# Autocorrelation beside key and value projections: two corrections moved from VectorE to GpSimd and ScalarE, and PSUM banks handed around

## The chip, the cores and the metric

The kernel runs on one core of one Trainium2 chip. A core has five engines with their own instruction queues: TensorE (PE, with PEld for its weight loads) multiplies matrices and writes to PSUM; VectorE (DVE), ScalarE (ACT) and GpSimd (POOL) work on data in SBUF, and the first two on PSUM as well; SyncE (SP) issues nearly all transfers here. PSUM has eight banks of 128 partitions by 512 fp32 numbers. Every engine takes its instructions in a fixed order and waits at an instruction until what it needs is there. The metric is the device time of one execution in microseconds. The kernel before takes 3332.24 us (median of three runs, 3330.26 to 3340.0).

## The reference

The input is `x` of 8 x 256 x 1024 and a context `ctx` of the same shape, all fp32. Four residual steps follow each other, each on the normalised `x` and each with a gate:

1. Autocorrelation attention of the normalised `x` (queries) with `ctx` (keys and values). For each of the 8 x 1024 columns: `corr = ifft(fft(q) * conj(fft(k))).real` along the 256 positions, the 11 largest lags with a softmax over them, and `out = sum_i w_i * v[min(lag_i + pos, 255)]`. A position that runs past the end reads the last position of `v`.
2. A linear layer with a low-rank update chosen per token among four ranks.
3. Grouped-query attention with rotary embedding (32 query heads, 8 key and value heads of 128), with keys and values projected from `ctx`.
4. A linear layer with a low-rank update through an orthogonal Fourier transform.

## The kernel before

The batch is done in two passes of four (`NPASS`, `BP`). A pass runs the autocorrelation with the key and value projections of step 3 beside it (in pass 0 also the folding of step 4's weights), then the linear layer of step 2 (`lora_ffn`), attention, and the last linear layer. In the profile the autocorrelation stages lie at 0 to 375 us (pass 0) and 1715 to 2060 us (pass 1).

**Autocorrelation.** `autocorrelation` (L383) treats 8 units per pass (4 sequences x 2 halves of 512 columns), one per call of `turn` (L472), and one more turn that only finishes. The transforms are matmuls with 128 x 128 matrices, after folding the 256 positions into sums and differences: `sums` (L448) makes `qe, qo` from the normalised x and `ke, ko` from the context `cn`, four adds on POOL (L460 to L463). The fold is written for a sequence shifted by one position, so the last position, which every overrun reads, counts too much: `end` (128 x 512, the last position of `ctx` broadcast to all partitions by a transfer, L445) is taken away from `ke` twice (L466, on DVE), and for the values it is put back in row 0 of the spectrum `kr` (L498, on DVE, one partition by 512). PE reads `ke` first at the start of the next turn (`dft`, L411).

A turn, in the order in which it is written: transfers for the next unit; spectra of `ke, ko`, copied from PSUM by ACT (`kr, kn, ki`); spectra of `qe, qo`, which `products` (L423) multiplies with the key spectra in four DVE instructions out of PSUM (L427 to L430) and joins in two POOL instructions (L431 to L435); the values' odd spectra, copied by ACT (`vr, vi`, L495 and L496); L498; then, for the unit of the turn before, eight transposes of its lag weights `both` on PE (L512, tiles `pt`), their copies `wt` by ACT, and two more rounds of spectra and `products` (`er, ei`, then `odr, odi`); `sums` for the next unit; and at the end the inverse transforms: `correlation` (L556) of this unit, `back` (L525) of the unit before (matmuls L531, added to x by DVE, L370), and `lags` (L567), which finds the largest lags on DVE (its masked weights, L583, read two SBUF tiles) and scales on ACT (L587). Two POOL instructions (L552, L553) make `both`.

**The work beside it.** `fill(n)` takes n steps of `keys_values` (L719): a step is eight matmuls of 128x128 by 256 (L796), half of one of the seven products of a Strassen form. A product is gathered in a bank of `ps_kv` and combined by DVE or ACT (`combine`, L223). A finished key tile is turned by `rope` (L709): three DVE instructions (L714 to L716), the first two into a tile `rope` of which there is one, then a POOL add (L717), then a store. In the first group of pass 0 the sums of weights (`wv_s`), and in later groups sums of the context (`cx_t`), are POOL adds too (L155, L159).

**PSUM.** In this stage: `ps_dft` 4 banks (spectra and `back`), `ps_cor` 1, `ps_out` 1 (the transposes `pt`), `ps_kv` 2, in all eight.

**Order.** The instructions of each engine are put in order by a planner when the program is built: the written order counts, but an instruction that the planner holds to be ready goes ahead of one that it holds not to be. The order is fixed before the program runs. On POOL, for instance, the adds of `sums` stand between those of `products`.

Of the kernel before, what the change touches and what calls it, by code (L numbers as in the profile page):

```python
# [11 lines left out]
F32 = mybir.dt.float32  # L12
U8 = mybir.dt.uint8
I32 = mybir.dt.int32
AF = mybir.ActivationFunctionType
ALU = mybir.AluOpType
AX = mybir.AxisListType
PSUM = bass.MemoryType.PSUM

P = 128  # L20
B, S, D = 8, 256, 1024
# [4 lines left out]
HALF = 512  # L26
# [20 lines left out]
def flamingo_kernel(ctx: ExitStack, tc: tile.TileContext, a: dict, out: bass.AP):  # L47
    nc = tc.nc
# [25 lines left out]
    tab_q = const.tile([P, 2, S], F32, name="tab_q")  # L74
# [306 lines left out]


    def autocorrelation(p, xt, pools, beside, late):  # L383
        c1, w1, w2, ps_dft, ps_cor, ps_out = pools

        def fill(n):
            for _ in range(n):
# [60 lines left out]
        def sums(b, cols, cn, end):  # L448

            xn = big_tile("xn", [2, HALF], "xn")  # L450
            for i, lin in enumerate(norms[b]):
                nc.scalar.activation(
                    xn[:, i, :],
                    xt[b * 2 + i][:, cols],
                    AF.Identity,
                    bias=lin[:, 1:2],
                    scale=lin[:, 0:1],
                )
            qe, qo, ke, ko = one("qe"), one("qo"), one("ke"), one("ko")
            nc.gpsimd.tensor_add(ke, cn[:, 0, :], cn[:, 1, :])  # L460
            nc.gpsimd.tensor_sub(ko, cn[:, 0, :], cn[:, 1, :])
            nc.gpsimd.tensor_add(qe, xn[:, 0, :], xn[:, 1, :])
            nc.gpsimd.tensor_sub(qo, xn[:, 0, :], xn[:, 1, :])  # L463


            nc.vector.scalar_tensor_tensor(ke, end, -2.0, ke, ALU.mult, ALU.add)  # L466
            return b, cols, end, qe, qo, ke, ko


# [2 lines left out]
        def turn(this, before, coming):  # L472


            after = None
            if this:
                b, cols, end, qe, qo, ke, ko = this
                if coming:
                    coming = loads(coming)
                kr_ps, ki_ps = dft((KCE, ke)), dft((KSE, ko), (NYQ, ke))  # L480


                kr, ki, kn = sb("kr"), sb("ki"), sb("kn")
                nc.scalar.copy(kr, kr_ps)
                nc.scalar.copy(kn, kr_ps)
                nc.scalar.activation(ki, ki_ps, AF.Copy, scale=pair)
                nc.scalar.copy(kn[0:1, :], ki_ps[0:1, :])
                re, im = sb("re"), sb("im")
                products(spectrum((CE, SE), (qe, qo)), kr, ki, kn, re, im, False)
                fill(2)  # L490

            if this:
                vr_ps, vi_ps = dft((KCO, ko)), dft((KSO, ke))
                vr, vi = sb("vr"), sb("vi")
                nc.scalar.copy(vr, vr_ps)  # L495
                nc.scalar.copy(vi, vi_ps)  # L496

                nc.vector.scalar_tensor_tensor(  # L498
                    kr[0:1, :], end[0:1, :], 2.0 * S, kr[0:1, :], ALU.mult, ALU.add
                )  # L500
                fill((1 if p == 0 else 2) if before else 6 if p == 0 else 2)
            last = not this
            if before:
                if last:
                    fill(3)
                b_cols, b_tiles, (bkr, bki, bkn, bvr, bvi, both) = before

                wt = []
                for t in range(2):
                    pt = ps_out.tile([P, HALF], F32, tag="out", name="pt")  # L510
                    for c in range(4):
                        nc.tensor.transpose(pt[:, c * P : (c + 1) * P], both[:, t, c, :], ident)  # L512
                    wt.append(one(f"wt{t}"))
                    nc.scalar.copy(wt[t], pt)
                    fill(2 if last else 1)
                er, ei = sb("re"), sb("im")
                products(spectrum((CE, SE), wt), bkr, bki, bkn, er, ei, True)
                fill(2 if last else 1)
                odr, odi = one("odr"), one("odi")
                products(spectrum((CO, SO), wt[::-1]), bvr, bvi, bvr, odr, odi, True)  # L520
                fill(3 if last else 2)
            if this and coming:
                after = sums(*coming)

            def back(l):  # L525


                if before:
                    po = ps_dft.tile([P, HALF], F32, tag="dft", name="po")
                    for i, (k, sp) in enumerate(((0, er), (3, odi)) if l else ((1, ei), (2, odr))):  # L530
                        nc.tensor.matmul(po, inv2[:, k, :], sp, start=(i == 0), stop=(i == 1))  # L531
                    residual(b_tiles[0][:, b_cols], po, tg_x[0])
                    residual(b_tiles[1][:, b_cols], po, tg_x[0] if l else ntg_x[0])
                    fill(1 - l)

            if last:
                back(0)
                back(1)
                return None, None
            w = big_tile("xn", [4, S], "w")  # L540
            cor = correlation(re, im, 0)
            fill(1)
            back(0)
            cor += correlation(re, im, 2)
            for c in range(2):
                lags(w[:, c, :], cor[c])
            fill(1)
            back(1)
            for c in range(2, 4):
                lags(w[:, c, :], cor[c])  # L550
            both = big_tile("xn", [2, 4, P], "both")
            nc.gpsimd.tensor_add(both[:, 0], w[:, :, 0:P], w[:, :, P:S])  # L552
            nc.gpsimd.tensor_sub(both[:, 1], w[:, :, 0:P], w[:, :, P:S])  # L553
            return after, (cols, xt[b * 2 : b * 2 + 2], (kr, ki, kn, vr, vi, both))
# [151 lines left out]
                pass  # L706


    def rope(dst, x, cos, sin, pool):  # L709

        H = P // 2
        t = pool.tile([P, 2, S], F32, tag="rope", name="rope", bufs=1)
        tab = lambda t: t.unsqueeze(1).to_broadcast([t.shape[0], 2, S])
        nc.vector.tensor_mul(t[0:H], x[H:P], tab(sin[H:P, :]))  # L714
        nc.vector.tensor_mul(t[H:P], x[0:H], tab(sin[0:H, :]))
        nc.vector.tensor_mul(dst, x, tab(cos))  # L716
        nc.gpsimd.tensor_add(dst, dst, t)  # L717

    def keys_values(n, groups, pools, tab):  # L719
# [3 lines left out]
        w1, w2, ps_kv = pools  # L723
# [57 lines left out]
        for u in range(4):  # L781
# [4 lines left out]
            for r in SEVEN:  # L786
# [16 lines left out]
                if done:  # L803
                    c, (i, j) = done
                    if kind == "wk":
                        kT = out_tile(c)
                        rope(kT, c, tab[:, 0, :], tab[:, 1, :], w1)
                        place = kT_d.rearrange("(q l i) p t -> q i p l t", l=2, i=2)
                        nc.sync.dma_start(
                            place[i_u, i, :, :, t0 + j * S : t0 + (j + 1) * S], kT  # L810
                        )
                    else:
                        r0, c0 = t0 + j * S, i_u * HALF + i * S
                        nc.sync.dma_start(
                            v_d[r0 : r0 + S, c0 : c0 + S].rearrange("(t p) d -> p t d", p=P), c
                        )
# [33 lines left out]
    def attention(p, xt, gq, go, keep, norms, xops, ahead):  # L850
        with (
# [115 lines left out]
            def queries(step, qT):  # L967

                wops, xo = wq[step], xops[step[0]]
                tiles = {}  # L970
                for r in SEVEN:
                    ps = ps_mm.tile([P, 2, S], F32, tag="mm", name="ps_q")
                    for l in range(2):
                        for c in range(KH):
                            nc.tensor.matmul(  # L975
                                ps[:, l, :],
                                wops[r][:, l, c, :],
                                xo[r][:, c, :],
                                start=(c == 0),
                                stop=(c == KH - 1),  # L980
                            )
                    done = combine(r, ps, tiles, lambda tag: half(tag, 1), lambda ps: ps)
                    if done:
                        qT[done[1]] = half("qT", 7)
                        rope(qT[done[1]], done[0], tab_q[:, 0, :], tab_q[:, 1, :], w1)
                    yield

            def outputs(step, ops):
# [209 lines left out]
            qT = {}  # L1198
# [5 lines left out]
            end = len(steps) - 1  # L1204
# [21 lines left out]
            for k, step in enumerate(steps):  # L1226
# [44 lines left out]
                qT = following  # L1271
# [76 lines left out]
    for p in range(NPASS):  # L1348
        ga, gb = ("a", "b") if p % 2 == 0 else ("b", "a")
        xt = [xpool.tile([P, D], F32, tag="x", name="x") for t in range(TT)]  # L1350
        with (
# [4 lines left out]
            tc.tile_pool(name="kv2", bufs=2, reuse_waits="tile") as kw2,  # L1356
            tc.tile_pool(name="ac_dft", bufs=4, space=PSUM) as ps_dft,
            tc.tile_pool(name="ac_cor", bufs=1, space=PSUM) as ps_cor,
            tc.tile_pool(name="ac_out", bufs=1, space=PSUM) as ps_out,
            tc.tile_pool(name="kv_ps", bufs=2, space=PSUM) as ps_kv,  # L1360
        ):

            tab = kw1.tile([P, 2, S], F32, name="tab")
# [15 lines left out]
            if p == 0:  # L1379
# [2 lines left out]
            autocorrelation(  # L1382
                p,
                xt,
                (c1, aw1, aw2, ps_dft, ps_cor, ps_out),
                steps,
                lambda: load_x(range(2, TT)),
            )
# [183 lines left out]
```

## Time and profile before

| | us |
|---|---|
| median of three runs | 3332.24 |
| the three runs | 3330.26, 3332.24, 3340.0 |
| the profiled execution | 3340.92 |
| its span, first to last instruction | 3339.1 |
| PE busy in it | 3267.4 |
| PE busy in 0 to 375, of 375 | 353.7 |
| PE busy in 1715 to 2060, of 345 | 326.2 |

A timeline line gives the start and the duration in us, the engine, the source line, the operation with output and inputs, the count, and in brackets the idle time of the engine before it with what ended it. "issue" there means that the profile shows nothing that was waited for. Of the windows view, a line gives the busy time (and number of instructions) of PE, PEld, DVE, ACT and POOL, then the granted PE clock, the busy share of the DMA engines and GB/s.

### The profile page before, as it was taken

The page shows a single profiled execution, that of the slowest core. Times are in us where ns is not written, and L with a number is a line of the kernel's source. Part 1 is how long each engine was busy: PE and PEld are TensorE (multiplying, and loading weights), DVE is VectorE, ACT ScalarE, POOL GpSimd, SP SyncE. Part 2 cuts the span into 40 slices and gives each one's busy share as a digit, 9 for nine tenths or more (in the row PEclk, how much of TensorE's full clock was granted, in tenths as well). Part 3 has the DMA queues.
Part 4 walks back from the last instruction along what each step waited for, and adds up shares of the span by engine and source line. Part 5 has one row for each costly group of instructions (what it writes and reads, how often), then busy time and mean ns, then how long its engine had stood idle before and what let it go on. Part 6 is the DMA issues. An engine that isn't in the chain of part 4 may idle for free. (4 is left out here: it accounts for less than half of the span.)

```text
span 3339.1 us, 39371 instructions
## 1 busy us (share of the span) xinstructions
PE 3267.4 (98%) x13456; PEld 2405.0 (72%) x13456; DVE 2221.3 (67%) x4305; ACT 1051.6 (31%) x2555; POOL 1404.9 (42%) x1181
## 2 busy tenths in 40 slices
PE   8999899999999999999999999999999999999999
PEld 6677456777677777775456677568888888888874
DVE  7787657777776655565647686456666767666773
ACT  1332111433333433334113332115343434334420
POOL 4554111323332474576344442112454454454572
PEclk9999999999999999999999999999999999999999
DMA  7534615333433354554354435043555455555551
GB/s 280 175 115 125 235 65 186 130 134 129 145 124 130 132 208 145 183 195 162 115 190 130 138 117 171 7 158 101 168 175 167 160 167 172 166 168 176 171 192 51
DMA packets 215781, 505.55 MB, mean 151 GB/s; under 512 B 25076, under 2 KB 102900, under 8 KB 215582
## 3 DMA queue, kind: packets, MB, share of 16 engines
q1 hardware_dynamic: 214430, 498.84, 44.2%
q0 software_dynamic: 1152, 4.19, 0.3%
q8 instruction: 108, 1.77, 0.2%
q14 instruction: 91, 0.75, 0.1%
HBM read 394.96 MB, written 108.00 MB: 151 GB/s over the span
## 5 line engine op out<-in xcount | busy, mean ns | idle before, releaser
L717 POOL TENSOR_TENSOR qT<-qT,rope 128x512 f32<-128x512 f32 x128 | 170.1, 1329 | 789.9 <-DVE qT L716 750.8
L975 PE MATMUL ps_q<-xn,wq 128*128 128x256 f32 x1920 | 428.9, 379 | 0.0
L975 PEld LDWEIGHTS ps_q<-xn,wq 128*128 128x128 f32 x1920 | 364.8, 190 | 50.5 <-PE po L677 0.5
L1145 ACT ACTIVATE s<-s,nmx 128x256 f32<-128x256 f32 x512 | 255.9, 500 | 245.0 <-DVE nmx L1142 244.8
L1140 DVE COPY_PREDICATED s<-keep,ps_s 128x512 f32<-128x512 uint8 x256 | 184.8, 727 | 156.0 <-PE ps_s L1131 155.1
L975 PE MATMUL ps_q<-xn_t,wq 128*128 128x256 f32 x1280 | 285.6, 379 | 0.0
L370 DVE SCALAR_TENSOR_TENSOR x<-po,tg,x 128x512 f32<-128x512 f32 x248 | 177.3, 743 | 139.3 <-PE po L1319 44.7
L975 PEld LDWEIGHTS ps_q<-xn_t,wq 128*128 128x128 f32 x1280 | 243.2, 190 | 33.1
L1172 ACT COPY wT<-pt 128x512 f32<-128x512 f32 x256 | 138.8, 586 | 361.8 <-PE pt L1166 361.8
L1131 PE MATMUL ps_s<-kT,qT 128*128 128x256 f32 x1024 | 247.9, 379 | 0.0
L1177 PE MATMUL av<-wT,v 128*128 128x256 f32 x1024 | 246.0, 382 | 1.7 <-ACT wT L1172 1.6
L1154 ACT ACTIVATE s<-s,tot 128x256 f32<-128x256 f32 x512 | 230.1, 497 | 40.6 <-DVE tot L1152 40.5
L1177 PEld LDWEIGHTS av<-wT,v 128*128 128x128 f32 x1024 | 191.4, 190 | 54.8 <-issue 22.2
L1067 PE MATMUL po<-wo,oI 128*128 128x256 f32 x896 | 214.7, 379 | 2.0 <-issue 1.2
L1131 PEld LDWEIGHTS ps_s<-kT,qT 128*128 128x128 f32 x1024 | 191.8, 190 | 25.1 <-issue 0.5
L1004 PE MATMUL po<-wo,oT 128*128 128x512 f32 x448 | 201.6, 593 | 0.0
L1067 PEld LDWEIGHTS po<-wo,oI 128*128 128x128 f32 x896 | 168.7, 190 | 25.6 <-issue 2.0
L1185 ACT COPY oT<-av 128x512 f32<-128x512 f32 x128 | 75.0, 586 | 353.9 <-PE av L1177 352.4
L1142 DVE TENSOR_REDUCE nmx<-s 128x2 f32<-128x512 f32 x256 | 173.2, 682 | 6.9
L1067 PE MATMUL po<-wo,oT 128*128 128x256 f32 x672 | 172.1, 382 | 1.9 <-DVE co L1082 0.3
L253 POOL TENSOR_TENSOR x<-x,part 128x512 f32<-128x512 f32 x48 | 68.3, 1423 | 247.1 <-ACT part L252 247.1
L1004 PEld LDWEIGHTS po<-wo,oT 128*128 128x128 f32 x448 | 83.0, 191 | 83.2 <-issue 74.8
(290 smaller groups left out, 6407.1 us busy)
## 6 DMA issues: line engine op xcount, KB each, us to landing
wo<-wo_d SPq DMA_DIRECT2D x144, 512.0 KB, 4.6
wq<-in_wq_dram SPq DMA_DIRECT2D x104, 512.0 KB, 3.5
wq<-wq_d SPq DMA_DIRECT2D x96, 512.0 KB, 3.3
wo<-in_wo_dram SPq DMA_DIRECT2D x56, 512.0 KB, 3.5
wo_d<-fine_t SPq DMA_DIRECT2D x56, 512.0 KB, 3.4
wo<-wo_d SPq DMA_DIRECT2D x96, 256.0 KB, 3.4
w<-w_d SPq DMA_DIRECT2D x36, 512.0 KB, 5.3
wo<-in_wo_dram SPq DMA_DIRECT2D x72, 256.0 KB, 3.3
```

The lines of the kernel that those rows point to most:

```text
L370: nc.vector.scalar_tensor_tensor(xs, ps, g, xs, ALU.mult, ALU.add)
L717: nc.gpsimd.tensor_add(dst, dst, t)
L975: nc.tensor.matmul(ps[:, l, :], wops[r][:, l, c, :], xo[r][:, c, :], start=(c == 0), stop=(c == KH - 1),)
L1004: nc.tensor.matmul(po, ops[r][:, h, t * P : (t + 1) * P], wops[r][:, h, :], start=(h == 0), stop=(h == 1),)
L1067: nc.tensor.matmul(po, left[r2][:, h, :], w[:, h, :], start=(h == 0), stop=(h == 1))
L1131: nc.tensor.matmul(ps[:, t, :], qT[i, n][:, l, t * P : (t + 1) * P], kT[:, n * S : (n + 1) * S], start=True, stop=True,)
L1140: nc.vector.copy_predicated(s, keep[b], ps)
L1142: nc.vector.tensor_reduce(nmx, s, AX.X, ALU.max, negate=True)
L1145: nc.scalar.activation(s[:, t, :], s[:, t, :], AF.Exp, bias=nmx[:, t : t + 1], accum_out=tot[:, t : t + 1],)
L1154: nc.scalar.activation(s[:, t, :], s[:, t, :], AF.Copy, scale=tot[:, t : t + 1])
L1172: nc.scalar.copy(wT[i], pt)
L1177: nc.tensor.matmul(av[:, i, :], kv[step][1][:, n * 2 + c, :], wT[i][:, c, :], start=(c == 0), stop=(c == 1),)
```

## The change

- The last position is taken away from `ke` by two instructions in place of L466: ACT scales `end` by -2 in place, and POOL adds it to `ke`. For row 0 of `kr`, in place of L498, ACT makes `back_end` (a new tile of 128 x 512, row 0 used) as `end` times -S, which is 2S times the position, and POOL adds it to row 0 of `kr`.
- The transposes `pt` get their banks from `ps_dft` (still 4 banks); `ps_out` is gone.
- `ps_kv` has three banks in place of two.
- `rope` takes the number of its buffers: two for the keys, one for the queries, as before.

The whole diff:

```diff
 def autocorrelation(p, xt, pools, beside, late):
-    c1, w1, w2, ps_dft, ps_cor, ps_out = pools
+    c1, w1, w2, ps_dft, ps_cor = pools
...
     nc.gpsimd.tensor_sub(qo, xn[:, 0, :], xn[:, 1, :])
-    nc.vector.scalar_tensor_tensor(ke, end, -2.0, ke, ALU.mult, ALU.add)
+    nc.scalar.activation(end, end, AF.Copy, scale=-2.0)
+    nc.gpsimd.tensor_add(ke, ke, end)
     return b, cols, end, qe, qo, ke, ko
...
     nc.scalar.copy(vr, vr_ps)
     nc.scalar.copy(vi, vi_ps)
-    nc.vector.scalar_tensor_tensor(
-        kr[0:1, :], end[0:1, :], 2.0 * S, kr[0:1, :], ALU.mult, ALU.add
-    )
+    back_end = one("back_end")
+    nc.scalar.activation(back_end[0:1, :], end[0:1, :], AF.Copy, scale=-1.0 * S)
+    nc.gpsimd.tensor_add(kr[0:1, :], kr[0:1, :], back_end[0:1, :])
...
     for t in range(2):
-        pt = ps_out.tile([P, HALF], F32, tag="out", name="pt")
+        pt = ps_dft.tile([P, HALF], F32, tag="dft", name="pt")
...
-def rope(dst, x, cos, sin, pool):
+def rope(dst, x, cos, sin, pool, bufs):
     H = P // 2
-    t = pool.tile([P, 2, S], F32, tag="rope", name="rope", bufs=1)
+    t = pool.tile([P, 2, S], F32, tag="rope", name="rope", bufs=bufs)
...
-        rope(kT, c, tab[:, 0, :], tab[:, 1, :], w1)
+        rope(kT, c, tab[:, 0, :], tab[:, 1, :], w1, 2)
...
-        rope(qT[done[1]], done[0], tab_q[:, 0, :], tab_q[:, 1, :], w1)
+        rope(qT[done[1]], done[0], tab_q[:, 0, :], tab_q[:, 1, :], w1, 1)
...
     tc.tile_pool(name="ac_dft", bufs=4, space=PSUM) as ps_dft,
     tc.tile_pool(name="ac_cor", bufs=1, space=PSUM) as ps_cor,
-    tc.tile_pool(name="ac_out", bufs=1, space=PSUM) as ps_out,
-    tc.tile_pool(name="kv_ps", bufs=2, space=PSUM) as ps_kv,
+    tc.tile_pool(name="kv_ps", bufs=3, space=PSUM) as ps_kv,
...
-        (c1, aw1, aw2, ps_dft, ps_cor, ps_out),
+        (c1, aw1, aw2, ps_dft, ps_cor),
```

## The prediction

> **What bounds the kernel now.** I read the page first: engines, then the windows of the stages, then PE's timeline inside them, then whoever ended its idle time.
>
> ```profile
> PE 3267.4 (98%) x13456; PEld 2405.0 (72%) x13456; DVE 2221.3 (67%) x4305; ACT 1051.6 (31%) x2555; POOL 1404.9 (42%) x1181
> ...
> 0.00:375.00 375.00, 353.70 (x1357) 256.70 (x1358) 274.64 (x668) 102.76 (x182) 181.61 (x149) 0.98 0.51 174
> 375.00:420.00 45.00, 35.11 (x119) 17.18 (x117) 37.88 (x84) 6.20 (x12) 1.26 (x1) 0.92 0.86 302
> 1715.00:2060.00 345.00, 326.22 (x1272) 239.54 (x1271) 247.75 (x616) 96.87 (x174) 159.12 (x125) 0.97 0.42 139
> ```
>
> PE is the bound: it works 98% of the span, and the change neither adds nor removes a matmul. So the change can only alter PE's idle time, 21.3 us in the first autocorrelation stage (375 - 353.7) and 18.8 in the second (345 - 326.2), and the matmuls that run slowly after an idle stretch. PE's timeline shows where:
>
> ```profile
> 77.76 3.75 PE L796 MATMUL ps_v<-wv,cx 128*128 128x256 f32 x8 [4.05 <-issue]
> ...
> 130.28 1.91 PE L411 MATMUL dft<-qo,mats 128*128 128x512 f32 x2 [5.06 <-DVE x L370]
> ...
> 219.53 1.99 PE L796 MATMUL ps_k<-cx,wk 128*128 128x256 f32 x8 [1.12 <-DVE k L716]
> ...
> 1732.56 6.43 PE L796 MATMUL ps_k<-cx,wk 128*128 128x256 f32 x16 [4.54 <-issue]
> ...
> 1781.71 3.07 PE L796 MATMUL ps_k<-cx,wk 128*128 128x256 f32 x8 [3.66 <-DVE k L716]
> ...
> 1906.05 3.78 PE L796 MATMUL ps_k<-cx,wk 128*128 128x256 f32 x8 [6.34 <-DVE v L244]
> ```
>
> Eight of these matmuls take 1.89 us elsewhere and sixteen 3.62, so an idle stretch of 3.7 us or more is paid again, in part, in slow matmuls; one of 1.1 (at 219.53) is not. The releaser is DVE, which frees the key and value banks. Why it was late is told by the correction L466 and one place in the timeline:
>
> ```profile
> L466 DVE SCALAR_TENSOR_TENSOR ke<-end,ke x16: 673/1215/6619, 26.0 to 1982.2; 128x512 f32<-128x512 f32 x16
> ...
>   POOL ke L460: 66.2, 15
> ```
>
> ```profile
> 1896.88 1.27 POOL L460 TENSOR_TENSOR ke<-cn 128x512 f32<-128x512 f32 x1
> ...
> 1898.18 6.62 DVE L466 SCALAR_TENSOR_TENSOR ke<-end,ke 128x512 f32<-128x512 f32 x1 [7.97 <-POOL ke L460]
> ...
> 1899.33 2.48 POOL L159 TENSOR_TENSOR cx_t<-cx,cx_t 128x512 f32<-128x512 f32 x2
> ...
> 1901.76 2.48 POOL L159 TENSOR_TENSOR cx_t<-cx_t,cx 128x512 f32<-128x512 f32 x2
> ...
> 1905.92 0.67 DVE L244 TENSOR_TENSOR v<-ps_v,u 128x512 f32<-128x512 f32 x1
> ```
>
> DVE stands at L466 for POOL, 66.2 us in 15 waits. Here it waits 7.97 us for `ke`, and then, with its input there, the instruction takes 6.62 us instead of 0.69, until POOL's run of adds is over. Behind it queue three combinations of `ps_v` that PE needs.
>
> **The change part by part.**
>
> *L466 leaves DVE.* DVE is freed of the 66.2 us of waits and of 24.4 us of L466 itself (its 16 durations added up). That time counts only where PE waited on it. At 1732.56 DVE had waited 10.65 us in L466 before the combination that frees the bank; at 1781.71, 3.64 us and then 1.76 in the instruction; at 1906.05 as quoted; at 219.53, 2.75 and 1.75. Without L466 each of these combinations is through before PE asks for the bank: at 1728.0 by 0.6 us (the product ends at 1724.6, L244 and the three rope instructions take 2.8), at 1778.05 by 1.8, at the others by more. Each stall is worth its idle time and what the next groups took over their normal spacing: 4.54 + 2.8 = 7.35; 3.66 + 1.8 = 5.45; 6.34 + 3.1 = 9.45; 1.12 + 0.1 = 1.2. Together 23.45.
>
> *Two rope buffers.* At 77.76 DVE had waited 6.32 us at L714 for POOL's L717, which still read the one rope tile and stood behind weight sums (POOL busy without a break from 66.9). With a second buffer DVE goes on at 69.2 and the bank is free: 4.05 + 2.5 = 6.5. But what is late next is POOL: its `ke` ends at 79.2, `ko` at 80.4, and the new add at 81.7 at the earliest, while PE would ask for `ke` at 85.42 - 6.5 = 78.9. So about 3.5 comes back as a wait for POOL, net 3.0.
>
> *The third key bank.* It lets one more product wait for its combination, about 3.5 us of PE work. Where the two items above free the bank in time it adds nothing; it widens the 0.6 us at 1728.0 and is the cover if DVE is still late. In the folding of pass 0, which uses the same banks, PE waits 0.38, 0.42, 1.12 and 2.0 for L326 (3.9 in all); I count nothing, since the DMA engines are 0.86 busy there, and keep 3.9 for the range.
>
> *The new POOL adds*, 32 of them. The ke adds cost 1.26 each by L460's row (same shape). For one partition by 512 no POOL row exists: DVE's L498 takes 0.71 to 0.80 when undisturbed, against 0.69 for 128 partitions, so partitions matter little; between nearly 0 and 1.26 I take 1.26, the row of the same engine. 40 us more on an engine with 181.6 of 375 and 159.1 of 345 busy. Does it lie beside other work? Each turn POOL idles before `both` (47.2 us in six waits in pass 1, 61.4 in pass 0) and usually waits for the next products before that, so there is room. `ke` is read at the earliest 6.2 us after L460 ends (1752.4 to 1758.64), in most turns 20 or more. The tight place is `odr`: the matmul L531 reads it 0.7 to 5.4 us after it is ready, under 2.8 in five turns of 16. Two adds in front (2.5) would overrun three of these, by 3.4 us in all (1.3, 1.8 and 0.2); but DVE's products come sooner by the wait removed. I take 0.5 for the turn at 1906, where POOL's run ends at 1904.24 and PE will come 9.45 earlier; and 0.3 at 1731.5, where `ke` ends between 1730.4 and 1731.7.
>
> *ACT.* 16 x 0.81 (L452's row, the same shape out of SBUF) and 16 x 0.56 (L487, 1 x 512): 22 us, at 31% busy. `end` landed a turn before. Behind the scaling on ACT stand only copies with several us in hand; if it were on the chain of lags to `both`, it would cost up to 0.8 per turn. I take 0. L498 gone from DVE is 19.1 us off it; nothing on PE waits for it. On SP the `cn` and `end` transfers keep their place.
>
> *Transposes in the spectra's banks.* Going round four banks, `pt` takes those of this turn's `qe, qo` spectra, so the first transposes wait until L429 and L430 have read these. In the trace L429 ends 2.3 us or more before the transposes in 12 of 14 turns, 0.17 before in one (1771.78), and 1.38 after in one (1815.50). The spectra after `pt` then wait for ACT's copies of `vr, vi`, long done. Between 0 and 2 us, I take 1.
>
> Sum: 23.45 + 3.0 - 0.5 - 0.3 - 1 = 24.65. Of pass 0's 4.2, half may be lost again at 375 to 420, where transfers limit: 22.5. The profiled execution (3340.92, span 3339.1) is the slowest of the four known, 8.7 over the median, and idle time in it may be larger than in the others; so I take 20 off the median: 3312.
>
> A rule against the change: the Trainium skill, "GPSIMD Engine Reference", section 4.1 Engine selection, puts elementwise adds on VectorE because GpSimd is about twice as slow. The rows agree on the ratio (1.26 against 0.69). Charged by it, the move would lose 32 x 0.57 = 18 us; by the trace L466 really held DVE for 90.6 us (66.2 + 24.4), and of POOL's time only the 3.5, 0.5 and 0.3 above reach PE, so I go by the trace. On the hold itself, "SBUF — State Buffer", section SBUF: two separate sides, says that a DVE instruction with two SBUF inputs and a GpSimd one lock each other out of a shared port for one whole instruction. By that L466 would lose at most 1.27; the trace has 6.62, through five POOL adds.
>
> That second place remains after the change in L583: it took 7.09 once (at 114.52, normally 0.42) and caused the stall at 130.28 (5.06 + 1.8). I leave that stall as it is; it could vanish (-6.8) or, with more POOL work, come again elsewhere (+6.8).
>
> **The rivals.**
>
> *Stalls move, nothing is gained.* POOL becomes the late engine: the planner puts the row-0 add before `both`, behind ACT's copies of `vr, vi`. From the turn at 212: the `vi` spectrum ends at 210.64, its copy and `back_end` at 211.8, the add at 213.1, `both` at 214.4, and the transposes start 2.2 us late; in pass 1, with one more step between, 0.5. 7 x 2.2 + 7 x 0.5 = 19, so 3332 - 20 + 19 = 3331. For it: POOL's order is the planner's. Against: re, im and L498 stand after `both` in the trace of before.
>
> *Slower: the cover runs out.* With three banks the planner runs key and value steps ahead of the autocorrelation, and the last turn of each pass has none left. A turn's own matmuls are about 19 us of its 36, so an uncovered turn idles up to 17, with some 5 of slow matmuls after it: 2 x 22 = 44 against 20 gained, 3356. It decides once 10 us per pass run dry. For it: the transposes are out of written order at 1817.98. Against: nearly everywhere else PE follows the written order, and pass 0 has the folding as cover.
>
> *More is gained:* the stall at 130.28 goes too, and the folding's 3.9: 3332 - 30 - 6.8 - 3.9 = 3291.
>
> **How the numbers follow.** Forecast 3312 (own range 3300 to 3322) 0.55; stalls moved, 3324 to 3342, 0.25; cover run out, 0.15; more gained 0.05. A difference under 0.3% (10 us) can't be told from none here. Faster: 0.55 x 0.95 + 0.05 + a tenth of the second = 0.60; slower: 0.15 and a tenth of the second = 0.18; same 0.22. The range goes from 3298 (all 30 and the folding's 3.9) to 3345, leaving out the cover's full price and the extreme gain.
>
> **What would show it.** No DVE wait for POOL of more than 2 us in a turn; DVE some 110 us less busy and waiting in the two stages; PE's idle gone near 1732, 1782 and 1906, and a wait for POOL's `ke` in the second turn of pass 0; POOL about 40 us and ACT 22 us busier. Wrong would be: PE waiting at the transposes for `both` in many turns, at L531 for `odr`, or idle at the end of a pass.

## The result and the profile after

The changed kernel takes 3354.38 us (median of four runs, 3350.98 to 3359.34) against 3334.19 for the kernel before (four runs, 3330.26 to 3340.0): a ratio of 1.0059, 95% interval 1.0043 to 1.0075, so 20 us slower where 20 us faster was forecast. The profiled execution of the changed kernel is the shortest of its four runs (3350.98, span 3349.2), that of the kernel before (3340.92) lies above all of its four, so the two traces differ by only 10 us. What sets one execution apart from the next is not shown by these profiles; the stages below are compared trace with trace.

The page and the windows of the changed kernel, in the columns used before:

```profile
PE 3267.8 (98%) x13456; PEld 2404.1 (72%) x13456; DVE 2180.9 (65%) x4273; ACT 1067.2 (32%) x2587; POOL 1435.7 (43%) x1213
```

```profile
0.00:375.00 375.00, 359.00 (x1376) 258.91 (x1376) 267.75 (x664) 110.42 (x198) 197.88 (x165) 0.99 0.52 177
...
1715.00:2060.00 345.00, 314.06 (x1213) 228.45 (x1212) 219.10 (x592) 104.30 (x189) 169.02 (x136) 0.96 0.38 130
```

PE's work is the same (3267.8 against 3267.4 us). In the first autocorrelation stage it is busy 359.0 of 375 instead of 353.7, which is a gain; in the second 314.1 of 345 instead of 326.2, a loss. The first key product of the second pass starts at 1712.09 instead of 1717.39, 5.3 us earlier; the transposes of its last turn start at 2058.60 instead of 2048.77. So 5.3 us were won by the start of the second pass, and 15.1 were lost within its autocorrelation stage; together they are the 10 us between the traces. PE's timeline of the changed kernel:

```profile
80.85 1.12 PE L411 MATMUL dft<-ke,mats 128*128 128x512 f32 x2 [2.87 <-POOL ke L467]
...
1756.70 1.13 PE L411 MATMUL dft<-ko,mats 128*128 128x512 f32 x2 [2.26 <-ACT kn L486]
...
1779.26 2.07 PE L411 MATMUL dft<-wt,mats 128*128 128x512 f32 x2 [8.52 <-ACT wt L515]
...
1823.48 1.55 PE L411 MATMUL dft<-wt,mats 128*128 128x512 f32 x2 [2.97 <-ACT wt L515]
...
1867.84 1.54 PE L411 MATMUL dft<-wt,mats 128*128 128x512 f32 x2 [4.48 <-ACT wt L515]
...
1916.52 2.07 PE L411 MATMUL dft<-wt,mats 128*128 128x512 f32 x2 [8.80 <-ACT wt L515]
```

None of the stalls shown of before at 1732, 1781 and 1906 is left, and the one at 78 has become a wait of 2.87 us for GpSimd's new add (now line L467). In their place PE waits for `wt`, the copies of the transposes by ScalarE: four long waits, 24.8 us together, and slow matmuls behind them. ScalarE in turn waits for a transfer, in the instruction that the change gave it:

```profile
L466 ACT ACTIVATE end<-end x16: 615/630/632, 26.5 to 1915.4; 128x512 f32<-128x512 f32 x16
...
  DMA end<-in_ctx_dram: 95.4, 14
```

ScalarE waits in the other new instruction too, `back_end` (L500), until GpSimd has read the one tile of that name:

```profile
L500 ACT ACTIVATE back_end<-end x16: 612/630/631, 27.2 to 1987.9; 1x512 f32<-1x512 f32 x16
...
  POOL kr L501: 42.0, 11
```

In the second pass only one short wait of PE, 0.74 us at 1819.38, ends at a `wt` that was copied after such a wait; the four long ones all end at a copy that stood behind the scaling.

The longest of these four, in the timeline of all engines:

```profile
1903.01 0.59 ACT L515 COPY wt<-pt 128x512 f32<-128x512 f32 x1 [2.29 <-PE pt L513]
...
1904.54 0.60 PE L513 MATMUL pt<-ident,both 128*128 128x128 f32 x4
...
1908.94 1.25 POOL L467 TENSOR_TENSOR ke<-ke,end 128x512 f32<-128x512 f32 x1
...
1910.21 0.34 SPq L445 DMA_DIRECT2D end<-in_ctx_dram  x1
...
1915.37 0.63 ACT L466 ACTIVATE end<-end 128x512 f32<-128x512 f32 x1 [11.77 <-DMA end<-in_ctx_dram]
...
1915.90 0.57 ACT L515 COPY wt<-pt 128x512 f32<-128x512 f32 x1
...
1916.52 2.07 PE L411 MATMUL dft<-wt,mats 128*128 128x512 f32 x2 [8.80 <-ACT wt L515]
```

ScalarE makes the first copy `wt` at 1903.0, and the second transposes are done at 1905.1. But between the two copies its order holds the scaling of `end`. That tile is being loaded for a unit two ahead of the one whose scaling is written at this place: its slot comes free when GpSimd has read the old `end` (L467, until 1910.19), SyncE issues the transfer at 1910.21, it lands some five microseconds later (3.8 to 6.0 in this pass), and only then do the scaling and the second copy run. Nobody needs the scaled tile then: this is the eighth scaling of the pass, and the eighth L467 reads it at 1992.82, 77 us later.

### The profile page after: what moved, and what is told of

The parts are those of the page before. It is cut to its first block, busy times and chain, and to the rows that moved or that the text cites. A ratio compares the mean times of both kernels' runs of the same rounds, so it can differ in the third digit from the quotient of the medians.

```text
span 3349.2 us, 39416 instructions
## 1 busy us (share of the span) xinstructions
PE 3267.8 (98%) x13456; PEld 2404.1 (72%) x13456; DVE 2180.9 (65%) x4273; ACT 1067.2 (32%) x2587; POOL 1435.7 (43%) x1213
## 4 chain that ended last, share of the span: by engine, by line
PE 81%; DVE 6%; POOL 3%; DMA 3%; issue 2%; ACT 1%; SPq 0%; DVEq 0%; POOLq 0%; ACTq 0%
PE ps_q L976 22%; PE po L1068 9%; PE po L1005 9%; PE ps_s L1132 6%; PE av L1178 6%; PE po L669 6%; PE po L1320 5%; PE ps_k L797 3%; PE ps_v L797 3%; PE pt L1167 3%; PE dft L411 3%; PE po L532 1%; DMA end<-in_ctx_dram 1%; PE pa L625 1%; PE pt L365 1%
## 5 line engine op out<-in xcount | busy, mean ns | idle before, releaser
L1132 PEld LDWEIGHTS ps_s<-kT,qT 128*128 128x128 f32 x1024 | 191.8, 190 | 25.1 <-issue 0.5
```

What stands on the lines that cost most here:

```text
L1132: nc.tensor.matmul(ps[:, t, :], qT[i, n][:, l, t * P : (t + 1) * P], kT[:, n * S : (n + 1) * S], start=True, stop=True,)
```

## The experiments

Theory A, after the result: the loss is the scaling's place in ScalarE's order. Theory B: the PSUM banks cost the time. Theory C: the GpSimd adds come too late whatever ScalarE does.

**Only the banks.** The changed kernel with both corrections on VectorE again.

```diff
-            nc.scalar.activation(end, end, AF.Copy, scale=-2.0)
-            nc.gpsimd.tensor_add(ke, ke, end)
+            nc.vector.scalar_tensor_tensor(ke, end, -2.0, ke, ALU.mult, ALU.add)
...
-                back_end = one("back_end")
-                nc.scalar.activation(back_end[0:1, :], end[0:1, :], AF.Copy, scale=-1.0 * S)
-                nc.gpsimd.tensor_add(kr[0:1, :], kr[0:1, :], back_end[0:1, :])
+                nc.vector.scalar_tensor_tensor(
+                    kr[0:1, :], end[0:1, :], 2.0 * S, kr[0:1, :], ALU.mult, ALU.add
+                )
```

> The changed kernel with both corrections put back on VectorE: only the banks (transposes in the spectra's banks, a third key bank) and the second rope buffer remain. Theory A (the scaling of `end` stands in ScalarE's order between the two copies `wt` and waits for its transfer, so PE waits for `wt`): no wait of PE for `wt` in the second pass, and the time lies between the kernel before and 20 us under it, 3315 to 3334, as the stalls at L466 stay but have one more bank. Theory B (the PSUM banks are what costs): the loss stays, 3345 or more. Theory C (the GpSimd adds themselves come too late): 3320 to 3335 like A, with no difference to A here.

Measured: 3315.05 us (before 3338.42 on the chip of the first four experiments), ratio 0.9933, 0.9917 to 0.9949. B falls. The gain is at the edge of what was expected, and it does not come from VectorE being free: the row of the correction in this kernel reads as before, with as much waiting for POOL (72.6 us against 66.2).

```profile
L466 DVE SCALAR_TENSOR_TENSOR ke<-end,ke x16: 673/1214/6634, 26.4 to 1955.7; 128x512 f32<-128x512 f32 x16
...
  POOL ke L460: 72.6, 15
```

VectorE is as late as ever, and the third bank lets PE go on. In the second pass one wait of PE for VectorE of more than a microsecond is left (1.18 us at 1886.83). This experiment keeps the second rope buffer; the sixth takes it away.

**Only the corrections.** The kernel before, with the corrections on ScalarE and GpSimd; the edit is the reverse of the last one, on the old banks.

> The kernel before with the corrections alone moved to ScalarE and GpSimd; banks and the rope buffer as before. A: the copies `wt` are again parted by the scaling in the second pass, PE waits some 25 us for them there: 3345 to 3360. B: no loss, 3310 to 3330. C: the loss is there as well, but PE's waits end at GpSimd instructions and not at `wt`.

Measured: 3360.77 us, ratio 1.0064, 1.0047 to 1.0082, just over the range of A. PE's timeline in the second pass:

```profile
1785.31 2.08 PE L411 MATMUL dft<-wt,mats 128*128 128x512 f32 x2 [5.89 <-ACT wt L515]
...
1825.34 1.22 PE L562 MATMUL ps_cor<-inv,re 128*128 128x256 f32 x2 [4.27 <-POOL re L431]
...
1876.18 2.08 PE L411 MATMUL dft<-wt,mats 128*128 128x512 f32 x2 [5.29 <-ACT wt L515]
...
1926.61 2.08 PE L411 MATMUL dft<-wt,mats 128*128 128x512 f32 x2 [9.44 <-ACT wt L515]
```

The waits for `wt` are there without the new banks. One of 4.27 us ends at GpSimd (`re`; 1.82 in the kernel before), which is what C looks for, but it is the smaller part.

**`end` loaded ahead of `cn`.** Two statements of `loads` exchanged in the changed kernel.

```diff
-            cn = w1.tile([P, 2, HALF], F32, tag="cn", name="cn")
-            nc.sync.dma_start(cn, a["ctx"][r0 : r0 + S, cols].rearrange("(s p) d -> p s d", p=P))
             end = w1.tile([P, HALF], F32, tag="end", name="end", bufs=2)
             nc.sync.dma_start(end, a["ctx"][r0 + P, cols].partition_broadcast(P))
+            cn = w1.tile([P, 2, HALF], F32, tag="cn", name="cn")
+            nc.sync.dma_start(cn, a["ctx"][r0 : r0 + S, cols].rearrange("(s p) d -> p s d", p=P))
```

> The changed kernel with the transfer of `end` issued ahead of that of `cn` (two statements of `loads` exchanged), so that it no longer queues on SyncE behind a transfer that waits for GpSimd; ScalarE's order is the same. A: ScalarE's waits for `end` shrink from up to 11.8 us to about 5 (the landing), PE's 25.5 us of waits for `wt` in the second pass to 5 to 12, the time to 3332 to 3346. B and C: unchanged within 5 us of the changed kernel, 3350 to 3358.

Measured: 3356.27 us, ratio 1.0059, 1.0042 to 1.0076: as the changed kernel, a miss for A. The trace tells why the edit tests nothing (the transfer of `cn` is L445 here, that of `end` L443):

```profile
1905.12 1.25 POOL L467 TENSOR_TENSOR ke<-ke,end 128x512 f32<-128x512 f32 x1
...
1905.17 0.38 SPq L445 DMA_DIRECT2D cn<-in_ctx_dram  x1
1906.39 0.34 SPq L443 DMA_DIRECT2D end<-in_ctx_dram  x1
...
1912.05 0.63 ACT L466 ACTIVATE end<-end 128x512 f32<-128x512 f32 x1 [12.25 <-DMA end<-in_ctx_dram]
```

SyncE's order did not change (the planner put `cn` first again), and `cn` was not what held `end` back: the slot was, which GpSimd frees at 1906.37.

**The scaling behind the copies.** The changed kernel with an edge of order, which makes ScalarE take the scaling after the second copy `wt` of the turn that is being written.

```diff
+        last_copy = [None]
...
-            nc.scalar.activation(end, end, AF.Copy, scale=-2.0)
+            with tc.issue_after(last_copy[0]) if last_copy[0] is not None else nullcontext():
+                nc.scalar.activation(end, end, AF.Copy, scale=-2.0)
...
-                    nc.scalar.copy(wt[t], pt)
+                    last_copy[0] = nc.scalar.copy(wt[t], pt).ins
```

> The changed kernel with the scaling of `end` kept behind both copies `wt` of the same turn in ScalarE's order (an edge of order only, no wait added). A: PE's waits for `wt` in the second pass are gone (25.5 us and the slow matmuls after them), and what was forecast for the freed VectorE shows: 3308 to 3328. B and C: 3345 or more.

Measured: 3315.51 us, ratio 0.9932, 0.9914 to 0.9950. Some 40 us for an edge that adds no instruction. The row of the scaling (L468 here) and a turn on ScalarE:

```profile
L468 ACT ACTIVATE end<-end x16: 612/632/643, 25.1 to 1953.2; 128x512 f32<-128x512 f32 x16
...
  DMA end<-in_ctx_dram: 15.1, 3
```

```profile
1760.77 0.59 ACT L517 COPY wt<-pt 128x512 f32<-128x512 f32 x1 [1.76 <-PE pt L515]
1762.94 0.59 ACT L517 COPY wt<-pt 128x512 f32<-128x512 f32 x1 [1.58 <-PE pt L515]
1763.42 0.63 ACT L468 ACTIVATE end<-end 128x512 f32<-128x512 f32 x1
1764.14 0.63 ACT L502 ACTIVATE back_end<-end 1x512 f32<-1x512 f32 x1
```

ScalarE waits 15.1 us for the transfer, three times, instead of 95.4, 14 times, and PE has no wait in the second pass between its first product and the transposes of the last turn. This shows A. B and C are out as the cause of the loss. In the second pass the edge moves the scalings back by two turns (the eighth stood between the copies of the fifth turn and now stands behind those of the seventh), and with them `back_end`, whose waits for GpSimd fall from 42.0 us to 0.6; by the timeline above these were not what PE waited for. Nothing else was edited, but the planner's order of the rest moves with it, as in every one of these kernels.

Why do the banks alone and everything together gain the same 23 us? Theory D: the third bank and the relief of VectorE cure the same stalls. Theory E: the relief is worth nothing.

**The corrections alone, with the edge.** The second experiment with the edit of the fourth.

> The corrections alone on ScalarE and GpSimd (banks and the one rope buffer as before), with the scaling kept behind both copies `wt`. Theory D (the two remedies overlap: VectorE's relief and the third bank each cure the same stalls of the second pass at 1732, 1781 and 1906): without the stalls of 22 us there, with those at 77 and 130 us left: 3308 to 3324. Theory E (VectorE's relief is worth nothing, the banks do all): 3328 to 3342, with PE still waiting for VectorE in the second pass.

Measured: 3321.07 us (before 3331.27 on the chip of this and the following experiments), ratio 0.9964, 0.9952 to 0.9977: the edge turns the second experiment's loss into a gain. With two key banks and one rope buffer PE's timeline has the stall of the rope tile left in the first pass, the one near 130 us does not come, and in the second pass there is none at VectorE:

```profile
78.46 3.75 PE L799 MATMUL ps_v<-wv,cx 128*128 128x256 f32 x8 [4.87 <-issue]
...
1799.86 1.06 PE L564 MATMUL ps_cor<-inv,re 128*128 128x256 f32 x2 [3.00 <-POOL re L432]
```

**The banks with one rope buffer.** The first experiment with `rope(..., w1, 1)` for the keys.

> The first experiment (corrections on VectorE, three key banks, transposes in the spectra's banks) with one rope buffer, as before. If the third bank is what cures the second pass: PE's second stage stays nearly free of waits and the time within 6 us of the first experiment, 3311 to 3324, with at most the stall at 77 us back. If the second rope buffer matters more: 3325 or more.

Measured: 3312.18 us, ratio 0.9941, 0.9928 to 0.9954. After its first product PE has no wait for VectorE in the second pass either, and none at 77: beside the third bank the second rope buffer adds nothing. Each remedy suffices by itself for VectorE's stalls of the second pass, which is D. In the time the relief alone gains 0.36%, the banks alone 0.59 to 0.67%, so the relief alone gains less in all: its stall at 78 and the wait of 3.00 us for `re` are left. Its trace, the shortest of its six executions, is only 2.5 us longer than that of the banks with one rope buffer; what sets its median 6 us above its trace is open.

**The rope buffer alone.** The kernel before with two rope tiles for the keys.

> The kernel before with a second rope buffer and nothing else. By the prediction's sum: the wait at 77 us (4.05 and 2.5 of slow matmuls) goes and about 3.5 comes back as a wait for `ke`, the stalls of the second pass stay: 3 us less than before, 3328 to 3338. If the rope buffer carries the gain of the banks: 3320 or less.

Measured: 3323.12 us, ratio 0.9979, 0.9969 to 0.9989, a gain of 7 us where 3 were expected. The stalls of the second pass stand where they stood in the kernel before:

```profile
1722.94 6.39 PE L796 MATMUL ps_k<-cx,wk 128*128 128x256 f32 x16 [4.51 <-issue]
...
1771.92 2.98 PE L796 MATMUL ps_k<-cx,wk 128*128 128x256 f32 x8 [3.63 <-DVE k L716]
...
1896.27 3.78 PE L796 MATMUL ps_k<-cx,wk 128*128 128x256 f32 x8 [6.36 <-DVE v L244]
```

The wait for `ke` that takes the place of the one at 77 us is 2.55 us. The second pass starts 9.6 us earlier (1707.81), and of this the stall at 130 us, which does not come in this kernel, is 6.8.

**Weight sums off GpSimd.** The fourth experiment, with the sums of one half of the value weights (first group of the first pass only) on VectorE.

```diff
-        def made_weight(kind, u, w):
+        def made_weight(kind, i, w):
...
-                eng = Short(nc.gpsimd if kind == "wv" else nc.vector)
+                eng = Short(nc.gpsimd if kind == "wv" and i == 0 else nc.vector)
```

> All of the change with the scaling behind the copies, and the sums of the second half of the value weights (the first group of pass 0 only) on VectorE in place of GpSimd. If the stall near 127 us (5.65 us and 1.8 of slow matmuls) comes from L583 being held on VectorE through GpSimd's run of weight sums: it goes, and the time is 4 to 8 us under the fourth experiment, 3306 to 3312. If not, or if VectorE is now late itself: 3313 or more.

Measured: 3308.31 us, ratio 0.9929, 0.9916 to 0.9942, the lowest time of all, but on another chip than the fourth experiment's. There the masked weights of `lags` (L586) had been held and PE had stalled behind them:

```profile
109.20 8.72 DVE L586 SCALAR_TENSOR_TENSOR w<-took,ex 128x256 f32<-128x256 f32 x1
```

```profile
126.59 2.04 PE L412 MATMUL dft<-qo,mats 128*128 128x512 f32 x2 [5.65 <-DVE x L370]
```

Here that instruction takes 0.41 to 0.42 us around that time, and the stall shrinks to 1.61 us:

```profile
123.48 1.12 PE L412 MATMUL dft<-qo,mats 128*128 128x512 f32 x2 [1.61 <-DVE x L370]
```

The interval overlaps that of the fourth experiment, so the step between the two is shown by the traces and not by the ratios.

The second pass in the traces, from PE's first key product to the transposes of the last turn:

| kernel | starts | ends | us |
|---|---|---|---|
| before | 1717.39 | 2048.77 | 331.4 |
| changed | 1712.09 | 2058.60 | 346.5 |
| only the banks | 1711.41 | 2022.11 | 310.7 |
| only the corrections | 1719.15 | 2068.64 | 349.5 |
| changed, scaling behind the copies | 1713.48 | 2019.72 | 306.2 |
| corrections, scaling behind the copies | 1708.00 | 2022.71 | 314.7 |
| banks, one rope buffer | 1710.08 | 2019.46 | 309.4 |
| rope buffer alone | 1707.81 | 2039.03 | 331.2 |
| `end` loaded ahead of `cn` | 1708.37 | 2056.66 | 348.3 |
| weight sums off GpSimd | 1708.74 | 2015.02 | 306.3 |

A trace is of one execution. That of the corrections with the scaling behind the copies is the shortest of its runs (3314.65, median 3321.07), as is that of `end` loaded first (3348.72, median 3356.27); that of the rope buffer alone (3331.69) lies 8.6 us above its median.

## Why the prediction was wrong

**ScalarE, the step that failed.** The prediction said of the scaling: "`end` landed a turn before. Behind the scaling on ACT stand only copies with several us in hand; if it were on the chain of lags to `both`, it would cost up to 0.8 per turn. I take 0." It took the place of the scaling from where it is written and from when its result is needed. But the scaling depends on the transfer alone, and the planner put it two units ahead, between the two copies of the transposes, before the transfer had landed; what it reckoned for the transfer is not on record. The price bounded was that of the instruction (0.81 by the nearest row; it took 0.63), not that of a wait for a transfer in front of the copies. On ScalarE the waits are 49.6 us in the second pass and 45.8 in the first; on PE four stalls of 24.8 us and, at 1756.70 and 1759.01, two of together 3.5 behind another scaling that waited 9.56 us: 28.2 us of idle time, and slow matmuls after it, where the sum had 0. In the first pass no scaling stands between the two copies of a turn, and its waits cost PE nothing that the trace shows.

**VectorE's relief: right.** The stalls at L466, counted at 23.45 us, go: with the edge, the corrections alone shorten the second pass by 16.7 us, and all of the change by 25.1, where the sum had 22.3 less some 2 of new waits. That the whole change with the edge gains some 23 us where 20 were forecast does not prove the sum, since the banks alone gain as much.

**Rope buffer and `ke`: right.** The 4.05 us at 77 became a wait for the new add, 2.87 where 3.5 was forecast. The buffer alone gained 7 us instead of 3, and by its trace most of that is the stall at 130 us, which was not counted for it: luck. The 5.3 us by which the second pass starts earlier likewise contain a smaller stall there (2.51 instead of 5.06).

**The third bank: worth more than the nothing that was counted.** By itself it cures the same stalls as the relief. On top of the relief, bank and rope buffer together bring 0.32% by the ratios (0.9964 and 0.9932), some 11 us, where 3.0 was counted for the two; in the second pass of the traces it is 8.5 us. The prediction called the bank a cover and did not see that it would do without the corrections, which in that company bring nothing that the times show (3315.05 against 3315.51).

**The GpSimd adds: right in price.** The one-partition add takes 1.26 us, the value taken; in the busy time GpSimd gained 30.8 us where 40 was forecast, ScalarE 15.6 where 22 was. `odr` came 0.99 us late once in the first pass (0.5 was taken, for another place); it is late there by 2.40 and 2.33 with the corrections on VectorE too (first and sixth experiment). Not counted was `re`: with the old banks PE's wait for it grew from 1.82 us to 4.27 and 3.00 (second and fifth experiment). **Transposes in the spectra's banks:** 1 us was taken; PE shows no wait of this kind.

**The hold on L583: came again.** It was left as a risk of 6.8 either way. In the changed kernel it held VectorE for 4.84 us at 114.85 and PE stalled for 2.51; with the edge 8.72 and 5.65.

**The rivals.** The slower one had the sign, not the mechanism: PE's last turns are covered (1.50 us at the end of the second pass, 1.51 before). GpSimd's row-0 add was not put in front of `both`. The case that decided, a wait for a transfer in the queue of an engine that is busy 31% of the time, was not among them.

## What to carry to other kernels

When a step moves to another engine, look at what its instruction waits for and not only at when its result is needed. Here the planner put an instruction that depends on a transfer alone two turns ahead of its use, and in a queue that keeps its order everything behind it waited for the transfer too. An edge of order to something late in the turn was the remedy. And where two remedies aim at one stall, run each alone before counting both: here a spare bank cured the stalls that relieving the late engine cured.

## What the runs showed of the hardware

A GpSimd add on one partition by 512 takes as long as one on 128 partitions by 512: 1.257 against 1.268 us (medians of 16). ScalarE's scaling takes 0.63 us for both shapes. And a VectorE instruction with two SBUF inputs was held for 8.72 us, from 109.20 to 117.92 (0.42 normally), while GpSimd's adds ran back to back until 117.64, the last four of them weight sums (fourth experiment); the longest holds in the trace of before are 7.09 and 6.62 us.
